# Last slots of a pixart block: maxima in the ring's banks, transposed scores over four banks, remainders last in a projection

## The chip, the core and the metric

The kernel runs on one core of one Trainium2 chip, in one launch. The metric is the time of one execution in device microseconds (us), and the median of several executions is given. The engines are TensorE (PE, whose loads of the stationary operand have a row of their own, PEld), VectorE (DVE), ScalarE (ACT), GpSimd (POOL) and SyncE (SP, which issues nearly all DMAs).

## The reference, cut to what matters

A transformer block over B = 16 batches of N = 256 tokens with H = 256 features, 16 heads of 16 features each, and an MLP of width 1024, all in float32:

```
x  = x + gate_a * (softmax(q k^T / 4) v @ W_proj + b_proj)      q, k, v from ln(x) @ W_qkv     "s"
x  = x + softmax(qc kc^T / 4) vc @ W_cproj + b_cproj            qc from ln(x), kc, vc from ln(context)   "c"
x  = x + gate_m * (gelu(ln(x) @ W_mlp1 + b_mlp1) @ W_mlp2 + b_mlp2)
```

The softmax of the reference subtracts the row's maximum. The kernel does so too, with a maximum taken over the tokens of each head.

## The kernel before, in words

Every projection splits each operand in a high and a low part and sums three products (high by high, high by low, low by high). The low part of an activation comes from a subtraction that follows the high part: for the attention's output `xTh_ac` is written by ACT, then `y_ac` (the unsplit copy) by ACT, then `xTl_ac` = `y_ac` - `xTh_ac` by POOL.

**Units, visits and beats.** The attention work is a list of 32 units: 16 of kind "s" and 16 of kind "c", one batch each. Units 28 to 31 are the context attentions of batches 12 to 15. `beat(n, k)` is the body of two nested loops, `n` from -1 to 31 and `k` from 0 to 7; in the text "visit (n, k)" is its first part, `visit(n, k, home)`. A visit does two things side by side. For unit n+1 it computes one token half of four heads' scores (`s_tile`, two partition halves `par` of 63 rows, 4 matmuls named `s<-big`), and DVE reduces their maxima into `mx` (`mx<-s`). For unit n it computes transposed scores of two heads (`t_part`, 4 matmuls named `st<-big`), and ACT exponentiates all four tiles in one instruction (`exp`, written to `pt`). The maxima are wanted as a 64th row of the stacked queries, so that the second matmul subtracts them: `m_part` transposes half of `mx` on PE (`psm`), ACT negates it into `m`, and SP sends it into `big`. That happens for unit n's second half at k = 0 and for unit n+1's first half at k = 4.

**PSUM.** There are eight banks. `sp` (two banks, the scores for the maxima) and `st` (two banks, the transposed scores) are fixed and single: the scores of a visit can't be written before the reduction of the visit before has read `sp`, nor the transposed scores before the `exp` of the visit before has read `st`. The other four are two rings of two: `LONG` (projections of the next units, later the MLP's first layer `ph`) and `SHORT` (everything brief: `psm`, the attention's output `o`, transposes `psA_c` and `psT_ac`, the output projection `psP_c`, and `ps_warm`, idle matmuls that `busy` puts in at given slots).

**The rest of a beat.** k = 0 and k = 4 run `av_part`, the product with the values (`o`, 32 matmuls). k = 2 and k = 6 transpose the output (`post.turn`, `psA_c`), `norm` divides by the row sum (DVE: reciprocal `rc_c`, then `A_c`), k = 4 transposes `A_c` (`psT_ac`) and makes the high part, k = 5 the low part. For the last four units (`whole = n > nu - 4`) the output projection is done in one piece, `p1.proj(0)` and `p1.proj(1)` at k = 6, with `end`, `add` and `store` at k = 7. Before, each call of `proj(t)` takes one token half, and in it the products follow one another as high-high, high-low, low-high for each of the two slices of the features. The last unit's projection runs in the MLP's loop instead, one call in each step (list `pst` after the loop over beats).

**The MLP.** It follows the attention, 16 batches of four chunks: `mlp_first` (`ph`, 12 matmuls), two gelus on ACT (`hf`, `hh`), a subtraction on POOL (`hl`), `mlp_second` (12 matmuls into `sp` or `st` by turns of the batch, named `s<-big,hh` and `st<-big,hh`). The first four chunks' `mlp_first` and the first batches' layer norms (`x`, `st_m`, `rs_m`, `xn_m`, `psT_m`, `xTf_m`) are put into the last attention beats.

Every engine's instructions are kept in program order, so the order on each queue is the one written out here. All calls go through one helper, so the profile gives line L51 for every operation; the names of the tiles tell them apart.

Of the kernel before, what the change touches and what calls it, by code (L numbers as in the profile page):

```python
# [16 lines left out]
P = 128  # L17
# [4 lines left out]
def pixart_block(  # L22
# [8 lines left out]
    B, N, H = x.shape  # L31
# [3 lines left out]
    NT = N // P  # L35
    KC = H // P
# [20 lines left out]
    PE = InOrder(nc.tensor, True)  # L57
# [7 lines left out]
    LONG, SHORT = "gen", "tr"  # L65
    ps_turn = [0]

    def ps_gen(name, tag=None):


        if tag is None and ps_turn[0] is not None:
            ps_turn[0] ^= 1
            tag = (SHORT, LONG)[ps_turn[0]]
        tag = tag or SHORT
        return psum.tile([P, 512], F32, tag=tag, name=name, bufs=2)
# [22 lines left out]
    def tok(ap, b):  # L98
        return ap[b].rearrange("(t p) h -> p t h", p=P)
# [33 lines left out]
    st = psum.tile([P, 2, 512], F32, tag="st", name="st", bufs=1)  # L133
    sp = psum.tile([P, 2, 512], F32, tag="s", name="s", bufs=1)
# [227 lines left out]
    def mm3_tok(dst, xT, t, W, kn=KC, start=True, stop=True):  # L362
        n = 0
        for k in range(kn):
            for a, b in ((xT[0], W[0]), (xT[0], W[1]), (xT[1], W[0])):
                PE.matmul(dst, a[:, k, t * P:(t + 1) * P], b[:, k],
                          start=(start and n == 0), stop=(stop and n == 3 * kn - 1))
                n += 1
# [120 lines left out]
    def bc_t(ap):  # L489
        return ap.unsqueeze(1).to_broadcast([P, NT, H])  # L490
# [25 lines left out]
    def build_post(u):  # L516

        b, name = u.b, f"{u.kind}{u.b}"
        W = Wp if u.kind == "s" else Wcp
        o = Box()  # L520

        def begin():
            if u.kind == "c":
                return
            G[b] = work.tile([P, 2, H], F32, tag="g", name=f"g_{b}", bufs=3)
            SP.dma_start(G[b].rearrange("p a h -> p (a h)"),
                         gd[b, 0:2].rearrange("a h -> (a h)").partition_broadcast(P))

        def gate():
            if u.kind == "c":  # L530
                return
            o.xg = work.tile([P, NT, H], F32, tag="xg", name=f"xg_{b}")
            POOL.tensor_tensor(o.xg, X[b], bc_t(G[b][:, 1]), ALU.add)

        def turn(hf):
            o.ps = ps_gen(f"psA{hf}_{name}", SHORT)
            for t in range(NT):
                for r in range(2):
                    PE.transpose(o.ps[:, (2 * t + r) * P:(2 * t + r + 1) * P],
                                 u.oT[hf][:, r, t * P:(t + 1) * P], ident)  # L540

        def norm(hf):
            if hf == 0:
                o.A = work.tile([P, NT, H], F32, tag="A", name=f"A_{name}", bufs=1)
            pv = o.ps.rearrange("p (x h c) -> p x h c", x=4, h=4)
            rc = work.tile([P, 4, 4, 1], F32, tag="rc", name=f"rc{hf}_{name}")
            DVE.reciprocal(rc, pv[:, :, :, HD:HD + 1])
            A = o.A.rearrange("p t (r f) -> p (t r) f", r=2)[:, :, 64 * hf:64 * hf + 64]
            DVE.tensor_tensor(A.rearrange("p x (h i) -> p x h i", h=4),
                              pv[:, :, :, 0:HD], rc.to_broadcast([P, 4, 4, HD]), ALU.mult)  # L550

        aT = transposed(lambda: o.A, f"a{name}", pool=True)

        def proj(t):
            if t == 0:
                o.ps = ps_gen(f"psP_{name}")
            mm3_tok(o.ps[:, t * H:(t + 1) * H], aT.xT, t, W)

        def end():
            t1 = work.tile([P, NT, H], F32, tag="t1", name=f"t1_{name}")  # L560
            o.t1 = t1
            ACT.copy(t1.rearrange("p t h -> p (t h)"), o.ps)

        def add():
            t1 = o.t1
            if u.kind == "s":
                POOL.tensor_tensor(t1, t1, bc_t(G[b][:, 0]), ALU.mult)
                X1[b] = work.tile([P, NT, H], F32, tag="x1", name=f"x1_{b}", bufs=5)
                POOL.tensor_tensor(X1[b], o.xg, t1, ALU.add)
            else:  # L570
                POOL.tensor_tensor(t1, t1, X1[b], ALU.add)
                o.out = t1

        def store():
            if u.kind == "c":
                SP.dma_start(tok(X2d, b), o.out)

        o.W, o.src, o.tok, o.name = W, aT, True, f"P_{name}"
        o.aT, o.begin, o.gate, o.turn, o.norm, o.proj, o.end, o.add, o.store = aT, begin, gate, turn, norm, proj, end, add, store
        u.post = o  # L580
        o.hurry = u.kind == "s" and b in (0, B - 1)
# [7 lines left out]
    def s_tile(u, g, par, t, bank=None, home=sp):  # L589

        alone = bank is None
        if alone:
            turn_of_s[0] ^= 1
            bank = turn_of_s[0]
        apart = isinstance(home, tuple)
        for j in range(2):
            PE.matmul((home[bank] if apart else home[:, bank])[:, j * N:(j + 1) * N],
                      u.q[par * 64:par * 64 + 63, 2 * g + j, t * P:(t + 1) * P],  # L600
                      u.k[par * 64:par * 64 + 63, 2 * g + j, :], start=True, stop=True)
            if j == 0:
                yield
        if u.mx is None:
            u.mx = work.tile([P, 2, 2, 4, NT], F32, tag="mx", name=f"mx_{u.n}", bufs=3)
        mx = u.mx.rearrange("p f r a t -> p r f a t")
        a = slice(2 * (g % 2), 2 * (g % 2) + 2)
        if alone or apart:
            src = home[bank] if apart else sp[:, bank]
            DVE.tensor_reduce(mx[:, par, g // 2, a, t], src.rearrange("p (j n) -> p j n", j=2),  # L610
                              AX.X, ALU.max)
        elif bank == 1:
            DVE.tensor_reduce(mx[:, :, g // 2, a, t], home.rearrange("p r (j n) -> p r j n", j=2),
                              AX.X, ALU.max)
        yield
# [8 lines left out]
            SP.dma_start(u.q[par * 64 + 63:par * 64 + 64, 4 * hf:4 * hf + 4, :].bitcast(F32),  # L624
                         m[par * 8:(par + 1) * 8].bitcast(F32))

    def t_part(u, pair, par):


        for c in range(NT):  # L630
            PE.matmul(st[:, par, c * N:(c + 1) * N],
                      u.k[par * 64:par * 64 + 64, pair, c * P:(c + 1) * P],
                      u.q[par * 64:par * 64 + 64, pair, :], start=True, stop=True)
            if c == 0:
                yield
        yield

    def exp(u, pair):
        u.pt[pair] = work.tile([P, 2, NT, N], F32, tag="pt", name=f"pt_{u.n}_{pair}", bufs=5)
        ACT.activation(u.pt[pair].rearrange("p r c n -> p (r c n)"), st.rearrange("p r n -> p (r n)"),  # L640
                       AF.Exp, scale=SCALE)

    later = []
# [7 lines left out]
    def in_turn(*pieces):  # L651

        for _ in range(2):
            for f in pieces:
                next(f)
# [23 lines left out]
    units = []  # L679
    for n, (kind, b) in enumerate(seq):  # L680
        u = Box()
# [5 lines left out]
    nu = len(units)  # L687
# [174 lines left out]
    for n, v in (("0", u0), ("1", u1), ("2", u2)):  # L862
        for c in "KQV":
            o = getattr(v, c)
# [8 lines left out]
    for n, v in (("0", u0), ("1", u1), ("2", u2)):  # L873
        word["T" + n + "t"], word["T" + n + "h"], word["T" + n + "l"] = v.T[0].parts
        word["T" + n + "p"] = v.T[0].low_pool
        for c in "KQ":
            o = getattr(v, c)
# [51 lines left out]
    def unit(n):  # L929
        return units[n] if 0 <= n < nu else None  # L930

    def visit(n, k, home=sp):


        v, e = unit(n + 1), k
        s = []
        if v:
            s = [s_tile(v, e // 2, par, e % 2, par, home) for par in range(2)]
        if n < 0:
            in_turn(*s)  # L940
            return
        t = [t_part(units[n], k, par) for par in range(2)]
        in_turn(*s)
        in_turn(*t)
        later.append(lambda: exp(units[n], k))

    def beat(n, k):
        if n < 0:
            visit(n, k, (st, sp)[k % 2])
            return  # L950
        cur, prev, nxt = unit(n), unit(n - 1), unit(n + 1)
# [22 lines left out]
        if k == 6 and q2:  # L974
            q2.V.keep()
        light = k == 6 and nxt and 3 < n < nu - 4 and not lx
        visit(n, k, (sp[:, 0], ps_gen("s1", SHORT)) if light else sp)
        if k == 0:
            if cur:
                m_part(cur, 1)  # L980
# [103 lines left out]
    for n in range(-1, nu):  # L1084
        ACT.on = E_['ON'][0] or n >= nu - 1
        for k in range(8):
            beat(n, k)
            for f in at[n, k]:
                f()
            if (n - nu, k) in W1P:  # L1090
                next(w1, None)
            if (n - nu, k) in W2P:
                next(w2, None)
            for q in (2 * k, 2 * k + 1):
                for f in at_end[n - nu, q]:
                    f()
# [3 lines left out]
    o = last.post  # L1100
# [78 lines left out]
```

## Time and profile before

| what | value |
|---|---|
| median of 3 runs | 810.0 us (808.59 to 810.6) |
| the profiled execution, its time | 807.08 us |
| its span, first to last instruction | 805.3 us |
| its mean granted TensorE clock | 0.999 |
| PE busy in the span | 781.0 us (97%) |
| DVE, ACT, POOL busy | 595.7, 584.9, 465.6 us |
| last units (about 560 to 621 us): PE busy | 53.72 of 61.00 us |

The profiled execution is 1.78 us longer than its span (start and end of the launch), and 2.9 us under the median of the runs. The visits that the change touches lie between 561 and 605 us, and the last unit's projection at 616 to 621 us. A row of the timeline gives the start, the time taken, the engine, the operation with its tiles, how many instructions were merged into it, and in brackets how long the engine sat idle before it and what ended that.

### The profile page before, as it was taken

To read this page: it belongs to the slowest core of one execution; us is meant where nothing else is said; L and a number is where in the kernel's file an instruction comes from. 1 tells how busy PE (TensorE), PEld (TensorE's weight loads), DVE (VectorE), ACT (ScalarE), POOL (GpSimd) and SP (SyncE) were. 2 spreads that over 40 slices of the span, in tenths; PEclk is the share of its full clock that TensorE was granted. 3 is DMA by queue.
4 is the path that set the end of the run, shared out by engine and by line. 5 is a ranking of instruction groups with operands and counts; after the bars stand their busy time and mean duration, and the time that the engine had idled before them with its cause. 6 is when DMAs were issued, how large, how long until landed. Compare 5 with 4: busy or idle time off the path is not lost.

```text
span 805.3 us, 23708 instructions
## 1 busy us (share of the span) xinstructions
PE 781.0 (97%) x9455; PEld 659.1 (82%) x9455; DVE 595.7 (74%) x1058; ACT 584.9 (73%) x1024; POOL 465.6 (58%) x405
## 2 busy tenths in 40 slices
PE   9999999999999999999999999999889999999997
PEld 8687777878877787877787787877568999999997
DVE  4887878788887878878888888876663666666662
ACT  3368878878888887888888888887556666666663
POOL 5755737574463756546475676663445666666653
PEclk9999999999999999999999999999999999999999
DMA  6554443435344443534445454534211312211311
GB/s 204 138 166 109 120 130 109 127 97 150 99 134 116 134 124 109 154 95 136 112 126 153 126 153 120 148 100 128 82 42 42 92 57 63 80 56 64 80 42 51
DMA packets 89939, 87.88 MB, mean 109 GB/s; under 512 B 9507, under 2 KB 85573, under 8 KB 89829
## 3 DMA queue, kind: packets, MB, share of 16 engines
q1 hardware_dynamic: 89364, 85.58, 38.0%
q8 instruction: 75, 1.23, 0.6%
q0 software_dynamic: 192, 0.52, 0.2%
q14 instruction: 36, 0.29, 0.1%
q10 hardware_dynamic: 272, 0.26, 0.1%
HBM read 26.97 MB, written 8.46 MB: 44 GB/s over the span
## 4 chain that ended last, share of the span: by engine, by line
PE 74%; DVE 11%; issue 5%; POOL 4%; ACT 4%; DMA 2%; SPq 0%; POOLq 0%; ACTq 0%
PE s L51 15%; PE o L51 13%; PE ph L51 11%; PE st L51 11%; DVE mx L51 8%; PE ps_qc L51 3%; PE ps_kc L51 3%; PE ps_q L51 3%; PE ps_P_s L51 2%; ACT pt L51 2%; PE ps_v_s L51 2%; PE psm L51 1%; PE ps_v_c L51 1%; PE ps_k L51 1%; PE ps_P_c L51 1%
## 5 line engine op out<-in xcount | busy, mean ns | idle before, releaser
L51 DVE TENSOR_REDUCE mx<-s 128x4 f32<-128x1024 f32 (+1 forms) x262 | 309.0, 1182 | 95.7 <-PE s L51 92.8
L51 ACT ACTIVATE pt<-st 128x1024 f32<-128x1024 f32 x256 | 261.1, 1020 | 45.4 <-PE st L51 38.7
L51 PE MATMUL s<-big 63*128 63x256 f32 x1008 | 120.2, 309 | 9.0 <-DVE mx L51 6.5
L51 PE MATMUL o<-pt,v 128*32 128x256 f32 x2048 | 123.8, 382 | 0.0
L51 POOL TENSOR_TENSOR hl<-hf,hh 128x512 fp32r<-128x512 f32 x64 | 88.7, 1395 | 55.7 <-ACT hh L51 54.7
L51 PEld LDWEIGHTS s<-big 63*128 63x128 f32 x1008 | 80.0, 185 | 43.8 <-DVE mx L51 22.7
L51 PE MATMUL st<-big 64*128 64x256 f32 (+1 forms) x1040 | 110.2, 284 | 3.6 <-ACT pt L51 3.6
L51 PEld LDWEIGHTS o<-pt,v 128*32 128x32 f32 x2048 | 60.0, 109 | 40.8
L51 PEld LDWEIGHTS st<-big 64*128 64x128 f32 (+1 forms) x1040 | 83.2, 186 | 8.2 <-ACT pt L51 6.1
L51 ACT ACTIVATE hf<-ph,bT 128x256 f32<-128x256 f32 x120 | 50.6, 474 | 27.8 <-PE ph L51 27.8
L51 ACT ACTIVATE hh<-ph,bT 128x256 fp32r<-128x256 f32 x120 | 50.5, 471 | 24.9 <-PE s L51 13.1
L51 ACT COPY oT<-o 128x512 f32<-128x512 f32 x63 | 37.0, 587 | 42.4 <-PE o L51 42.4
L51 POOL TENSOR_TENSOR xTl_c<-y_c,xTh_c 128x512 fp32r<-128x512 f32 x16 | 20.5, 1281 | 60.2 <-PE s L51 52.0
L51 POOL TENSOR_TENSOR xTl_as<-y_as,xTh_as 128x512 fp32r<-128x512 f32 x16 | 20.5, 1278 | 56.1 <-ACT y_as L51 56.1
L51 PE MATMUL ph<-wqch,wself 128*128 128x256 f32 x256 | 51.8, 285 | 0.0
L51 PE MATMUL ph<-wkch,wself 128*128 128x256 f32 x256 | 51.8, 286 | 0.0
L51 POOL TENSOR_TENSOR xTl_ac<-y_ac,xTh_ac 128x512 fp32r<-128x512 f32 x16 | 20.5, 1280 | 54.0 <-ACT y_ac L51 50.1
L51 PE MATMUL s<-big,hh 128*128 128x256 f32 x256 | 47.4, 282 | 0.0
L51 PE MATMUL st<-big,hh 128*128 128x256 f32 x256 | 47.2, 281 | 0.0
L51 DVE TENSOR_SCALAR xn_m<-x,mv_m,rs_m 128x256 f32<-128x256 f32 x32 | 38.3, 1235 | 11.4 <-POOL rs_m L51 11.4
L51 PEld LDWEIGHTS ph<-wqch,wself 128*128 128x128 f32 x256 | 42.0, 191 | 0.4 <-issue 0.4
L51 PEld LDWEIGHTS ph<-wkch,wself 128*128 128x128 f32 x256 | 41.9, 191 | 0.4
(222 smaller groups left out, 2379.0 us busy)
## 6 DMA issues: line engine op xcount, KB each, us to landing
big<-h_kc SPq DMA_DIRECT2D x64, 128.0 KB
big<-h_qc SPq DMA_DIRECT2D x64, 128.0 KB
big<-h_k SPq DMA_DIRECT2D x62, 128.0 KB
big<-h_q SPq DMA_DIRECT2D x62, 128.0 KB
big<-l_k SPq DMA_DIRECT2D x32, 128.0 KB
big<-l_q SPq DMA_DIRECT2D x32, 128.0 KB
c<-in_ctx_dram SPq DMA_DIRECT2D x16, 256.0 KB
g<-gd SPq DMA_DIRECT2D x16, 256.0 KB
```

The costliest lines, as they stand in the source:

```text
L51: i = f(*a, **k)
```

## The change

There are three edits.

1. Maxima: in every second visit from (29, 7) on, namely (29, 7), (30, 1), (30, 3), (30, 5) and (30, 7), the two tiles of scores go into the two `LONG` banks instead of `sp`. With two separate tiles the reduction is done by two instructions of 128x512 in place of one of 128x1024 (`apart` in `s_tile`).
2. Transposed scores: in the last unit (n = 31, which has no scores for maxima beside it), odd visits write to `sp` and even ones to `st`, and `exp` reads that bank.
3. Whole projections: `proj(0)` now does the eight matmuls with the high part for both token halves, and `proj(1)` the four with the low part, as one accumulation group in the bank. It applies to units 28, 29 and 30 (at k = 6 of the beat after) and 31 (in the MLP's loop: `proj(0)` before `mlp_second` of chunk 2, `proj(1)` after it).

```diff
-        def proj(t):
-            if t == 0:
+        def proj(half):
+
+            if half == 0:
                 o.ps = ps_gen(f"psP_{name}")
-            mm3_tok(o.ps[:, t * H:(t + 1) * H], aT.xT, t, W)
+            for t in range(NT):
+                for k in range(KC):
+                    for a, b in (((1, 0),) if half else ((0, 0), (0, 1))):
+                        PE.matmul(o.ps[:, t * H:(t + 1) * H], aT.xT[a][:, k, t * P:(t + 1) * P], W[b][:, k],
+                                  start=(half == t == k == b == 0), stop=(half == 1 and t == NT - 1 and k == KC - 1),
+                                  skip_group_check=True)
...
+        bank = sp if n == nu - 1 and k % 2 else st
+        t = [t_part(units[n], k, par, bank) for par in range(2)]
...
+        later.append(lambda: exp(units[n], k, bank))
...
-        visit(n, k, (sp[:, 0], ps_gen("s1", SHORT)) if light else sp)
+        home = sp
+        if light:
+            home = sp[:, 0], ps_gen("s1", SHORT)
+        elif nxt and n * 8 + k >= nu * 8 - 17 and k % 2:
+            home = ps_gen("s0", LONG), ps_gen("s1", LONG)
+        visit(n, k, home)
```

`t_part` and `exp` take the bank as an argument `st` that stands for the tile of that name.

More of the change, by code (lines that the diff above doesn't have):

```diff
@@ L625, in m_part, with t_part @@
                          m[par * 8:(par + 1) * 8].bitcast(F32))
-    def t_part(u, pair, par):
+    def t_part(u, pair, par, st):
         for c in range(NT):
@@ L636, in t_part, with exp @@
         yield
-    def exp(u, pair):
+    def exp(u, pair, st):
         u.pt[pair] = work.tile([P, 2, NT, N], F32, tag="pt", name=f"pt_{u.n}_{pair}", bufs=5)
@@ L941, in visit @@
             return
-        t = [t_part(units[n], k, par) for par in range(2)]
+        bank = sp if n == nu - 1 and k % 2 else st
+        t = [t_part(units[n], k, par, bank) for par in range(2)]
         in_turn(*s)
         in_turn(*t)
-        later.append(lambda: exp(units[n], k))
+        later.append(lambda: exp(units[n], k, bank))
     def beat(n, k):
```

## The prediction

> **What bounds the kernel now.** I read the page's busy row first, then busy time by stretch, then PE's waits in the stretch that the change touches, then the timeline there.
>
> ```profile
> 100.00:540.00 440.00, 433.78 (x6138) 347.85 (x6128) 364.04 (x627) 362.73 (x581) 256.81 (x223) 1.00 0.45 125
> 560.00:621.00 61.00, 53.72 (x523) 41.85 (x521) 35.14 (x71) 36.37 (x55) 28.89 (x24) 1.00 0.20 61
> 621.00:806.00 185.00, 179.13 (x1484) 176.25 (x1482) 105.87 (x196) 110.26 (x262) 108.65 (x86) 0.99 0.22 64
> ```
>
> The columns are the stretch, its length, then busy us of PE, PEld, DVE, ACT and POOL, PE's granted clock, DMA share and GB/s. PE is full in the attention (434 of 440) and in the MLP (PE ends at 800.4; until then the waits show 0.2 us of idle PE and 2.9 us of PEld). Only the last units have holes, 7.3 us. What PE gains there therefore reaches the end.
>
> ```profile
> engine line waited for: us in total, times, longest us
> PEld s L51 <- DVE mx L51: 4.1, 5, 1.4
> PEld psP_c L51 <- POOL xTl_ac L51: 2.8, 4, 1.4
> PEld st L51 <- ACT pt L51: 2.2, 2, 1.4
> ```
>
> These are PEld's waits from 561 to 621 us: scores wait for the reduction that frees `sp`, projections for the remainder, transposed scores for the exponential that frees `st`. Together 9.1 us, and each edit aims at one row. The timeline says how much of each is real gain:
>
> ```profile
> 564.80 0.40 PE L51 MATMUL st<-big 64*128 64x256 f32 x4
> 566.29 0.57 PE L51 MATMUL s<-big 63*128 63x256 f32 x4 [1.09 <-DVE mx L51]
> 566.63 0.46 PE L51 MATMUL st<-big 64*128 64x256 f32 x4
> ...
> 574.06 0.40 PE L51 MATMUL st<-big 64*128 64x256 f32 x4
> 575.70 0.50 PE L51 MATMUL s<-big 63*128 63x256 f32 x4 [1.24 <-DVE mx L51]
> 576.04 0.40 PE L51 MATMUL st<-big 64*128 64x256 f32 x4
> ...
> 593.72 0.50 PE L51 MATMUL st<-big 64*128 64x256 f32 x4 [0.59 <-ACT pt L51]
> ...
> 616.59 0.28 PE L51 MATMUL psP_c<-wcpl,xTh_ac 128*128 128x256 f32 x1
> 618.07 0.38 PE L51 MATMUL psP_c<-wcph,xTl_ac 128*128 128x256 f32 x1 [1.20 <-POOL xTl_ac L51]
> ```
>
> Behind each delayed `s` stands an `st`, and that needs the exponential of the visit before, which releases almost as late:
>
> ```profile
> 565.30 1.02 ACT L51 ACTIVATE pt<-st 128x1024 f32<-128x1024 f32 x1 [2.20 <-PE st L51]
> 574.56 1.02 ACT L51 ACTIVATE pt<-st 128x1024 f32<-128x1024 f32 x1 [0.91 <-PE st L51]
> ```
>
> It starts 0.50 after its `st` and takes 1.02; the next `st` starts 0.05 later (586.54 to 586.59). From `st` to `st` that makes 1.57, where the reduction makes 1.83 (564.80 to 566.63) and 1.98.
>
> **Edit 3, remainders last.** Twelve matmuls come 0.12 apart. Now the third waits; afterwards the ninth does, 0.72 later.
> - Unit 28 (562.3): second matmul 562.52, third 563.07 where 562.64 was possible, and a restart takes 0.22 to the next instead of 0.12. The remainder ends at 563.03, the ninth is due at 563.36. Gain 0.43 + 0.10 = 0.53.
> - Unit 29 (582.4): 583.29 against 582.77, 0.62 in full. But PE will by then be 2.0 early (below), and the remainder is not: POOL must first do the split `big<-w` (1.27) that follows a cast on DVE, which I find only 0.86 early. POOL then ends the remainder near 581.6, the ninth is due at 581.5. Gain 0.40.
> - Unit 30 (602.3): 603.00 against 602.66, plus 0.10: 0.44.
> - Unit 31 (616.5): 618.07 against 616.71, plus 0.10: 1.46. In place of the wait stand six matmuls and `mlp_second` of chunk 2, whose `hl` ends at 616.79 and is thus in time; the remainder is needed only after it.
>
> Sum 2.83. Nothing is added on any engine.
>
> **Edit 1, maxima.** DVE pays for five pairs:
>
> ```profile
> L51 DVE TENSOR_REDUCE mx<-s 128x4 f32<-128x1024 f32 x242 | 296.1, 1223 | 95.6 <-PE s L51 92.8
> L51 DVE TENSOR_REDUCE mx<-s 128x2 f32<-128x512 f32 x20 | 12.9, 686 | 0.0
> ```
>
> Ten such pairs are in the trace already (20 instructions, 12.9 us): 1.29 a pair against 1.22, so 0.07 more. [...]
>
> Place by place, with the saving carried forward (0.53 from unit 28):
> - (30, 0): `s` goes at once, `st` waits for the exponential: 1.57 in place of 1.83, gain 0.26. Then `psm` takes the bank that `A_c` frees. On DVE `A_c` ends 1.84 after the reduction's start, 1.91 with a pair, about 566.4; PE would be there at 566.2. Loss 0.15. Saved so far 0.64.
> - (30, 2): idle 0.22 before `s` goes, and the exponential (570.16 to 571.18) frees `st` before 571.26. Gain 0.22, so far 0.86.
> - (30, 4): 1.98 becomes 1.57, gain 0.41, so far 1.27. `psm` needs the pair of (30, 3): DVE is 0.86 early, so it ends at 573.57 + 1.29 = 574.86; `psm` is due at 575.10.
> - (30, 5): the reduction before was held up behind `st_m<-x`, which waits for POOL. PEld idles 0.68 before `s`, of which 0.17 is issue after transposes: gain 0.51, so far 1.78.
> - (30, 6): 0.22, so far 2.00; with unit 29's projection 2.40.
> - (31, 0): the wait of 1.17 for the exponential stays (even visit, same bank). `psm` waits for `A_c` here too: loss 0.07.
>
> Sum 1.40 of the row's 4.1. The ring is free: its last user, `v<-ps_v_c`, ends at 562.15. New on PE's path is the landing of `l_qc` for the first scores of unit 31: the trace has it at 563.90, `s` of (30, 0) will want it at 564.6. The row `m` of (30, 4) landed at 573.73 with its issue now 0.5 earlier; wanted at 574.8. No gap either way: at 0 here, and if the landing were 1 us later, 0.3 and 0 lost.
>
> **Edit 2, four banks.** Only (31, 3) waits among the odd and later visits: PEld idle 0.83, gone in full, as `sp`'s exponential (31, 1) ended 4 us before. So far 2.33 + 0.83 = 3.16. What is late next? `psT_m` of batch 1 at 598.85 needs `xn_m`, at the end of a chain: `x2d<-t_c` on SP 588.56, two `m` DMAs behind it, `x<-x2d` 590.43, POOL `x` 593.17, `st_m`, `rs_m`, `xn_m` ending 597.21. It starts from unit 29's projection, so it moves 2.33 to 594.9; PE arrives at 595.7. Margin 0.8, cost 0.
>
> **Sum.** 2.83 + 1.40 + 0.83 = 5.06, say 5.1 us. The profiled execution would go from 807.08 to 802.0. The median of the runs stands 2.9 above that execution, and I carry the saving over: 810.0 - 5.1 = 804.9.
>
> TensorE's clock: the trace grants 1.0 from 4.2 to 802.9 us and 0.5 from there, 2.5 after the last matmul (800.4). Waits up to 1.2 cost no clock; the change shortens them. [...]
>
> **The rivals.**
> - *The chain to `xn_m` does not move* (its DMA is bound by something else on SP's queue). Then `psT_m` goes at 597.25, not 595.7: 1.6 lost, 3.5 gained, 806.5. For it: a chain of waits that follows exactly these steps up to `xn_m` at 596.4. Against: each step in it is released by the one before, none by a clock of its own. Chance 0.10.
> - *Waits only change names:* exponentials take the maxima's place fully (gain 0 of 1.40), (31, 3) passes its 0.83 on to `o`, and unit 31's 1.46 is given back to the gelus, whose `hh` is what `ph` of the next batch waits for. Left 1.4, 808.6, no change that can be told: a measurement here tells 0.3%, 2.4 us. Against: `hh` of chunk 5 waits for `mlp_second` of chunk 2, which comes earlier too. Chance 0.05.
> - *Slower:* one transfer that PE meets earlier, the `x<-x2d` of batch 1, lands late among others. Its place is `psT_m` in (31, 4). A wait past 2.5 us would also drop the clock to 0.5, as at the end; the record has the full clock only from 4.2 us after the start, so I estimate half of that, 2 us, for a drop. It turns the sum negative when `xn_m` comes over 3.1 later than before (597.2): wait 1.6 + 3.1 = 4.7, plus 2, against 5.1; at 5 later, 1.6 + 5 + 2 - 5.1 = 3.5 slower, 813.5. Against: DMA share there is 0.10 to 0.36. Chance 0.05.
> - That edit 1 does nothing is excluded: the program has the five pairs in those visits.
>
> **Numbers.** My case has 0.80: 804.9, with its own range 803.3 to 806.2 (DVE's and POOL's lateness up to 1.3 worse; landings and waits up to 1.6 better, short of the 9.1 less the 1.4 that stays). With the first rival and the runs' scatter of 1 us: 803.0 to 807.5. Faster by over 0.3%: 0.80 + 0.10 = 0.90; same 0.05; slower 0.05.
>
> **What would show it.** In the profile after, between 561 and 621 us: PEld's waits for `mx` gone but for some tenths; its waits for `pt` up to 2.5, at (30, 0), (30, 4) and (31, 0); for `xTl_ac` under 0.4; the first `psT_m` after the last projection at 615.7 in place of 620.8; pairs of 0.69 in five visits. Wrong would be: `psm` waiting over 0.5 for DVE, `psT_m` of batch 1 waiting for `xn_m`, a granted clock under 1.0 before 795, or an MLP that doesn't start earlier.

## The result and the profile after

The median went from 809.27 us (6 runs, 808.59 to 810.6) to 804.81 us (6 runs, 802.47 to 805.27); the ratio is 0.9941 with a 95% interval of 0.993 to 0.9953. The forecast was 804.9. An execution with a low mean granted clock (one of edit 3 alone had 0.853 and took 844.89 us) is left out of all ratios here. The profiled execution took 804.78 us with a span of 803.0 us, only 2.3 less than the one before. Which of the two numbers is the change's? The exponentials of one visit ahead of the first edit give the answer, first before and then after (timelines of ACT):

```profile
562.07 1.02 ACT L51 ACTIVATE pt<-st 128x1024 f32<-128x1024 f32 x1
```

```profile
564.46 1.03 ACT L51 ACTIVATE pt<-st 128x1024 f32<-128x1024 f32 x1
```

This is visit (29, 6). The execution after reached it 2.39 us later, with the same program up to there; the exponentials of units 27 to 29 stand 2.38 to 2.45 apart, and 1.1 of it is there at the first exponential. It is what two executions differ by in their first 500 us, and belongs to no edit. So I measure the **tail**: from that exponential to the end of the last matmul. It is 238.29 us before (562.07 to 800.37) and 233.58 after (564.46 to 798.04): 4.71 us less, near the 4.46 that the medians differ by. Up to the last projection the tail tells executions apart to a few hundredths (where two versions have the same code, they agree to 0.01), and at its end to about 0.1, which a time with 2 us of scatter can't.

Busy time by stretch after (columns as in the prediction; moved by the 2.39, the stretch that was 560 to 621 before would be 562.4 to 618.7, which has the same holes as the second row):

```profile
100.00:540.00 440.00, 433.90 (x6133) 348.28 (x6129) 363.19 (x625) 362.82 (x582) 254.95 (x223) 1.00 0.45 125
560.00:616.00 56.00, 52.42 (x535) 40.58 (x528) 36.64 (x79) 35.03 (x50) 25.07 (x22) 1.00 0.24 74
616.00:806.00 190.00, 181.83 (x1507) 178.96 (x1505) 105.85 (x196) 113.23 (x270) 112.32 (x89) 0.99 0.21 62
```

PE's holes in the last units shrank from 7.3 to 3.6 us. Of the three rows of PEld's waits from 561 to 621 us one remains (sum, number, longest):

```profile
PEld st L51 <- ACT pt L51: 3.7, 3, 1.4
```

And one of PE's own waits in the same stretch, with the same columns:

```profile
PE psm L51 <- DVE A_c L51: 0.3, 2, 0.2
```

The rows for `mx` (4.1) and `xTl_ac` (2.8) are gone, and the one for `pt` grew from 2.2 to 3.7, with three waits, two of them new. The timeline of PE shows where:

```profile
566.89 0.41 PE L51 MATMUL s<-big 63*128 63x256 f32 x4
568.24 0.50 PE L51 MATMUL st<-big 64*128 64x256 f32 x4 [0.94 <-ACT pt L51]
568.91 0.27 PE L51 MATMUL psm<-ident,mx 128*16 128x128 f32 x1 [0.17 <-DVE A_c L51]
...
577.37 0.50 PE L51 MATMUL st<-big 64*128 64x256 f32 x4 [0.94 <-ACT pt L51]
577.80 0.28 PE L51 MATMUL psm<-ident,mx 128*16 128x128 f32 x1
...
586.82 0.50 PE L51 MATMUL st<-big 64*128 64x256 f32 x4 [1.18 <-ACT pt L51]
...
593.32 0.50 PE L51 MATMUL s<-big 64*128 64x256 f32 x4
...
616.46 0.28 PE L51 MATMUL psP_c<-wcpl,xTh_ac 128*128 128x256 f32 x1
...
618.02 0.64 PE L51 MATMUL psP_c<-wcph,xTl_ac 128*128 128x256 f32 x4
618.50 0.60 PE L51 MATMUL psT_m<-ident,xn_m 128*128 128x128 f32 x4
```

At (30, 0) and (30, 4) `s` goes at once, and `st` behind it waits 0.94 where `s` had waited 1.09 and 1.24: most of the maxima's wait only moved one instruction on. At (31, 3) the transposed scores, now in `sp` and so named `s` (593.32), wait for nothing, and neither does the last unit's remainder (618.02), with `mlp_second` ahead of it. The last row is the start of the MLP's steady part. It came at 620.81 before, which is 623.20 with the 2.39 added; so 4.70 of the 4.71 are there by then, and the MLP passes them on to the end.

### The profile page after: what moved, and what is told of

It is laid out like the page before. It is cut to its first block, busy times and chain, and to the rows that moved or that the text cites. A ratio compares the mean times of both kernels' runs of the same rounds, so it can differ in the third digit from the quotient of the medians.

```text
span 803.0 us, 23712 instructions
## 1 busy us (share of the span) xinstructions
PE 781.8 (97%) x9455; PEld 660.3 (82%) x9455; DVE 596.0 (74%) x1063; ACT 584.8 (73%) x1024; POOL 465.4 (58%) x405
## 4 chain that ended last, share of the span: by engine, by line
PE 79%; DVE 9%; ACT 4%; POOL 3%; issue 3%; DMA 1%; ACTq 0%; POOLq 0%; SPq 0%
PE s L51 17%; PE o L51 14%; PE ph L51 11%; PE st L51 11%; DVE mx L51 7%; PE ps_qc L51 3%; PE ps_kc L51 3%; PE ps_q L51 3%; ACT pt L51 2%; PE ps_P_s L51 2%; PE ps_v_s L51 2%; PE ps_v_c L51 2%; PE psm L51 2%; PE ps_k L51 1%; PE ps_P_c L51 1%
## 5 line engine op out<-in xcount | busy, mean ns | idle before, releaser
L51 ACT ACTIVATE pt<-st 128x1024 f32<-128x1024 f32 x252 | 257.0, 1020 | 40.3 <-PE st L51 34.1
L51 PE MATMUL s<-big 63*128 63x256 f32 (+1 forms) x1024 | 122.1, 309 | 6.5 <-DVE mx L51 3.6
L51 PEld LDWEIGHTS s<-big 63*128 63x128 f32 (+1 forms) x1024 | 81.2, 185 | 41.6 <-DVE mx L51 19.0
```

Of the source, the lines that this page charges most:

```text
L51: i = f(*a, **k)
```

## The experiments

All savings below are from the tail of one profiled execution of each version, place by place: the start of the exponential of a visit, counted from that of (29, 6), in us earlier than before. The rows are cumulative.

| saved by the start of | after | edit 3 alone | edit 1 alone | edit 2 alone | `norm` early | flipped | both |
|---|---|---|---|---|---|---|---|
| exp (29, 7) | 0.53 | 0.53 | 0.00 | 0.00 | 0.53 | 0.53 | 0.53 |
| exp (30, 0) | 0.51 | 0.54 | -0.02 | 0.00 | 0.74 | 0.51 | 0.74 |
| exp (30, 4) | 0.96 | 0.53 | 0.43 | 0.00 | 1.20 | 0.95 | 1.20 |
| exp (30, 6) | 1.61 | 0.52 | 1.08 | 0.00 | 1.84 | 1.60 | 1.84 |
| exp (30, 7) | 2.17 | 1.16 | 0.94 | 0.00 | 2.40 | 2.15 | 2.39 |
| exp (31, 0) | 2.12 | 1.15 | 0.88 | 0.00 | 2.58 | 2.10 | 3.05 |
| exp (31, 3) | 2.78 | 1.15 | 0.88 | 0.66 | 3.24 | 2.77 | 3.39 |
| exp (31, 7) | 3.23 | 1.60 | 0.87 | 0.67 | 3.68 | 3.21 | 3.83 |
| last projection done | 4.69 | 3.06 | 0.87 | 0.66 | 5.14 | 4.67 | 5.29 |
| last matmul done | 4.71 | 3.05 | 0.78 | 0.66 | 5.13 | 4.66 | 5.28 |

**Edit 3 alone** (the kernel before with the new `proj`):

```diff
-        def proj(t):
+        def proj(half):
...
-            mm3_tok(o.ps[:, t * H:(t + 1) * H], aT.xT, t, W)
+            for t in range(NT):
+                for k in range(KC):
+                    for a, b in (((1, 0),) if half else ((0, 0), (0, 1))):
```

> Only edit 3 (remainders last). The tail is measured from the exponential of visit (29, 6) to the end of the last matmul: 238.3 us before, 233.6 with all three edits, 4.7 less. Theory (each projection's wait is real gain, nothing behind it gives it back): 0.53 + 0.62 + 0.44 + 1.46 = 3.05 us less in the tail, so 235.25; unit 29 gains its full 0.62 here, since PE is only 0.53 early there and POOL's remainder moves by as much. Time about 806.2 against 809.3. Rival (waits only change names: what units 28 to 30 save is lost again at the next wait for maxima or exponentials): 1.5 us less, 236.8. In the rows: waits of PEld for xTl_ac gone, those for mx (4.1) and pt (2.2) as before.

Median 806.46 against 809.48, ratio 0.9962 (0.9948 to 0.9977), 3.1 us less by the ratio. The rows are those of another execution, profiled at a mean granted clock of 0.998:

> The same kernel with edit 3 alone, for a profile at full clock. Theory: 3.05 us less in the tail (235.25) with steps of 0.53, 0.62, 0.44 and 1.46 at the four projections. Rival (lost again at the next wait): 236.8, with steps that vanish at (30, 0) and (31, 0).

Its tail is 3.05 us shorter, with steps of 0.53, 0.63, 0.44 and 1.46. The waits for `mx` (4.1) and `pt` (2.2) are unchanged. The theory holds, the rival falls: these four waits, with nothing behind them that another engine holds back, are gain in full.

**Edit 1 alone** (the kernel before with the new `home`):

```diff
-        visit(n, k, (sp[:, 0], ps_gen("s1", SHORT)) if light else sp)
+        home = sp
...
+        elif nxt and n * 8 + k >= nu * 8 - 17 and k % 2:
+            home = ps_gen("s0", LONG), ps_gen("s1", LONG)
+        visit(n, k, home)
```

> Only edit 1 (maxima of every second visit in the ring). Theory: the after trace shows 1.15 us gained at (30, 0) to (30, 6) and a loss of 0.04 at (31, 0); alone, unit 29's projection stands in the way, because its third matmul waits for a remainder that ACT's y_ac allows only about 0.9 earlier. So 0.9 us less in the tail, between 0.7 and 1.1: 237.4. Time about 808.4. Rival (exponentials take the place of the maxima fully): 0.3 or less. Rival (maxima are worth the 1.4 forecast): 1.4. In the rows: PEld's wait for mx from 4.1 to under 0.5, its wait for pt from 2.2 to about 4, the wait for xTl_ac larger than 2.8 by 0.2 to 0.5.

The tail is 0.87 shorter at the last projection and 0.78 at the end, within the 0.7 to 1.1. The times can't tell it: ratio 0.9995 (0.9984 to 1.0007). PEld's waits in this run:

```profile
PEld st L51 <- ACT pt L51: 4.5, 4, 1.4
PEld psP_c L51 <- POOL xTl_ac L51: 3.0, 4, 1.4
```

The wait for `mx` (4.1 before) is gone, and 2.3 of it is back under `pt`. At unit 29's projection 1.08 falls to 0.94, where the third matmul waits for its remainder: this is why edit 1 is worth 0.97 by (31, 0) beside edit 3 (2.12 against the 1.15 of edit 3 alone) and 0.88 without. In unit 30 itself it is worth 1.08 in both.

**Edit 2 alone:**

```diff
+        bank = sp if n == nu - 1 and k % 2 else st
+        t = [t_part(units[n], k, par, bank) for par in range(2)]
...
+        later.append(lambda: exp(units[n], k, bank))
```

> Only edit 2 (transposed scores over four banks in the last unit). Theory: the 0.67 us that the after trace shows at (31, 3) come alone as well, since everything behind starts from PE: 0.67 less in the tail, 237.6; time about 808.6, hard to tell from no change by the clock, but the tail tells it. Rival (the chain that ends in xn_m of batch 1, or the wait for o, takes it back): under 0.2 less. In the rows: PEld's wait for pt from 2.2 to 1.4, the one at (31, 0) left.

The tail is 0.66 shorter, all of it at (31, 3), and nothing gives it back. The ratio, 0.9993 (0.9981 to 1.0006), can't tell. The wait for `pt` fell from 2.2 to 1.4, the one at (31, 0). The three edits alone make 3.05 + 0.78 + 0.66 = 4.49, together 4.71; at the last projection, ahead of the MLP's scatter, it is 4.59 against 4.69.

**What holds psm: `norm` early, the banks flipped, both.** In the changed kernel `psm` at (30, 0) and (31, 0) waits for `A_c`, whose bank of the `SHORT` ring it takes. `norm` early:

```diff
+        if k == 7 and cur and whole:
+            cur.post.norm(0)
         home = sp
...
-            if cur:
+            if cur and not whole:
                 cur.post.norm(0)
```

> The changed kernel, with norm(0) of units 29 to 31 issued ahead of the scores of visit (n, 7) instead of behind its reduction: the bank that psm waits for is then free earlier. Theory: psm of (30, 0) and (31, 0), which the after trace shows waiting 0.17 for A_c behind pairs of reductions, goes right after its st: 0.34 and 0.33, so 0.67 less in the tail than the changed kernel (233.6 to 232.9); time about 804.1. Rival (psm waits for the pair itself): 0.1 or less at (30, 0), where the pair ends at 568.14 and st starts at 568.24.

Tail 233.17 (5.13 less), so 0.42 more, 0.23 at each place where 0.34 and 0.33 were expected; median 804.26, ratio 0.9935 (0.9916 to 0.9954). The wait was real, its size off by 0.1: behind an `st` that has waited itself, `psm` follows 0.43 later (587.05 to 587.48 here), not 0.33 as behind one that hadn't.

```diff
-        bank = sp if n == nu - 1 and k % 2 else st
+        bank = sp if n == nu - 1 and k % 2 == 0 else st
```

> The changed kernel, with the banks of the last unit the other way round (sp in even visits, st in odd ones), so that the transposed scores of (31, 0) need not wait 1.18 for the exponential of (30, 7). Theory: the wait moves from st to psm, which A_c holds at the same place: the tail stays at 233.6 within 0.1, although the largest wait of PEld for pt is gone. Rival (the exponential is the bound): 1.2 less, 232.4.

Tail 233.63, 0.05 longer than the changed kernel's; median 804.63. The timeline of PE around (31, 0):

```profile
584.89 0.39 PE L51 MATMUL s<-big 64*128 64x256 f32 x4
586.90 0.27 PE L51 MATMUL psm<-ident,mx 128*16 128x128 f32 x1 [1.62 <-DVE A_c L51]
```

The transposed scores (now in `sp`) wait for nothing, and `psm` 1.62 instead. A wait of 1.18 was taken away and bought nothing: the next one, of `psm` for `A_c`, ends where it did.

> Both: norm(0) early and the banks flipped. Theory: at (31, 0) psm is then held by the pair of reductions alone, which ends 0.76 before psm starts now: 0.72 there and 0.34 at (30, 0), 1.06 less in the tail than the changed kernel (232.5), more than the 0.67 and 0.0 of the two alone; time about 803.7. Rival (the parts add up): 0.67 if the exponential does not matter, 1.9 if it does.

Tail 233.01, 0.57 less than the changed kernel's; median 804.1, ratio 0.9932 (0.991 to 0.9955). The same place:

```profile
583.54 0.40 PE L51 MATMUL s<-big 64*128 64x256 f32 x4
584.84 0.28 PE L51 MATMUL psm<-ident,mx 128*16 128x128 f32 x1 [0.90 <-DVE mx L51]
585.36 1.93 PE L51 MATMUL o<-pt,v 128*32 128x256 f32 x32 [0.24 <-ACT t_c L51]
```

`psm` is held by the pair of reductions, as expected, and starts 0.94 earlier than in the changed kernel (where it gained 2.12 on before, here 3.06). But 0.32 of it is lost in the next instruction, which takes the bank that ACT's copy `t_c` of the projection reads. So the two together gain more than apart (0.57 against 0.42 - 0.05), less than the 1.06 forecast.

**The idle matmuls.** Groups of `ps_warm` fill PE at five slots of units 30 and 31. Without them:

```diff
-... (30, 0): 'd3', (30, 1): 'd2', (30, 2): 'd3', (30, 5): 'd3', (31, 1): 'd2'
```

> The changed kernel without the idle matmuls ps_warm of (30, 0), (30, 1), (30, 2), (30, 5) and (31, 1): 26 matmuls, 3.7 us of PE, whose output nothing reads. Theory (with the maxima's wait gone, unit 30 is held by the chain of exponential, reduction and psm, not by PE): only about 1.4 of the 3.7 come back, 0.8 by (31, 0) and 0.6 at (31, 1); tail 232.2, time about 803.4; waits of PEld for pt and of psm for DVE appear in unit 30. Rival (PE is the bound there): 3.7 less, 229.9. Rival (the idle matmuls hold the clock): granted clock under 1.0 in some stretch from 565 to 600 us and a time that is no better.

Up to (31, 0) the tail is 3.07 shorter than before, 0.95 more than in the changed kernel: the chain of exponential, reduction and `psm` keeps the rest, as the theory said. Then more than that gain goes. The timeline of PE:

```profile
587.02 3.62 PE L51 MATMUL o<-pt,v 128*32 128x256 f32 x32
```

And the busy time in the 5 us around it (columns as above; the granted clock is the third from the end):

```profile
585.00:590.00 5.00, 3.69 (x36) 1.83 (x37) 3.69 (x7) 2.67 (x4) 2.61 (x3) 0.71 0.16 53
```

The 32 matmuls `o` take 3.62 in place of 1.93, and the granted clock in those 5 us is 0.71; the trace has it at 0.5 from 587.1 to 590.5. By (31, 1) the saving is 1.40, and the tail ends at 234.01, 0.43 longer than the changed kernel's. The second rival is right for this execution as far as its signs go; whether the missing groups did it is another matter, since the 3.4 us ahead of the fall hold none of the five slots (last section). (Median 804.19, ratio 0.9935, 0.9915 to 0.9956.)

On top of `norm` early and the flip, three groups taken out, then all five:

```diff
-(30, 0): 'd3', (30, 1): 'd2', (30, 2): 'd3'
```

> The version with norm(0) early and the banks flipped (tail 233.0, 5.3 less than before), and without the idle matmuls of (30, 0), (30, 1) and (30, 2); those of (30, 5) and (31, 1) stay. Theory: as in the run without any of them, the chain of unit 30 gives back about 0.9 of their 2.3 us, and with the waits of (31, 0) gone the clock stays at 1.0: tail 232.1, time about 803. Rival (unit 30's waits let the clock fall, as in that run): a stretch at 0.5 between 565 and 595 us, tail 233.5 or more.

Again the clock fell, earlier: 0.5 from 575.7 to 579.2. The busy time around that:

```profile
575.00:580.00 5.00, 4.05 (x40) 1.94 (x39) 3.51 (x9) 2.08 (x3) 3.20 (x3) 0.66 0.06 18
```

The saving was 2.00 at (30, 3) and 1.37 at (30, 5); tail 233.39, no better than with the groups (233.01). Median 803.63, ratio 0.9919 (0.9894 to 0.9944).

> The same without any of the five groups of idle matmuls. Theory: 0.6 more at (31, 1): tail 231.5, time about 802.4, if the clock holds. Rival (it does not hold, as in the run without them): a stretch of 3.4 us at 0.5, which costs 1.7, tail 233.2, and runs that spread more widely than those of the other versions.

Here the clock held in the profiled execution (1.00 in each stretch of 5 us from 560 to 605, 0.999 in the mean), and the theory's number came out: tail 231.50, 6.79 less than before and 2.08 less than the changed kernel. The median is 802.5, ratio 0.9921 (0.9894 to 0.9947), the lowest median here, though the version with three groups out has the same ratio (0.9919); its eight runs spread from 800.78 to 808.32, over 7 us, where the changed kernel's spread over 2.8. By the times it isn't told apart from the changed kernel (the intervals overlap).

How often does the clock fall? The mean granted clock of a whole execution is 0.997 in both profiled ones where it fell and 0.998 to 1.0 in the others profiled at full clock, so I take 0.997 or less for the sign of a fall; that is my estimate from these means. It was recorded for 9 of the 20 runs of the three versions with groups left out and for 2 of the 25 of the four changed versions with all groups, but also for 13 of the 53 of the kernel before and for 5 of the 11 of edit 1 alone, which have all groups too. So by this sign a fall is likelier without the groups than in the changed versions with them, but they don't exclude it.

## Why the prediction was right

That the median was forecast to 0.1 us is luck: the median of before that I started from was 0.7 above the one it was compared with (810.0 against 809.27), and the saving was forecast 0.6 above what the medians gave (5.06 against 4.46), so the two errors cancelled. What can be judged are the terms, which add to 5.06 against 4.71 in the tail. Term by term, with every visit's exponential counted as in the table's column "after":

| term | forecast | measured |
|---|---|---|
| remainder, unit 28 | 0.53 | 0.53 |
| (30, 0): wait moved, less `psm` | 0.26 - 0.15 | -0.02 |
| (30, 2) | 0.22 | 0.14 |
| (30, 4) | 0.41 | 0.31 |
| (30, 5) | 0.51 | 0.51 |
| (30, 6) | 0.22 | 0.14 |
| remainder, unit 29 | 0.40 | 0.56 |
| (31, 0), `psm` | -0.07 | -0.05 |
| (31, 3), four banks | 0.83 | 0.66 |
| remainder, unit 30 | 0.44 | 0.44 |
| remainder, unit 31 | 1.46 | 1.46 |

- **Remainders**: exact where nothing else moves. Unit 29's was 0.16 better than forecast: PE was only 1.61 early at that point, not 2.0, so of the 0.22 that I had charged for POOL's lateness 0.07 showed (0.56 against 0.63 with edit 3 alone).
- **Maxima**: the mechanism was the one forecast (`st` waits for the exponential instead, `psm` for `A_c`), the sizes 0.1 too kind at four places. At (30, 0) I let `psm` start as `A_c` ends; in the profile after it starts 0.15 later (568.76 to 568.91). At (30, 4) the cost is the 0.43 from a waiting `st` to `psm` against 0.33. At (30, 2) and (30, 6) I had the exponential free `st` in time; it ended 0.05 ahead of `st` (573.70 and 573.75 at (30, 2)), which is the distance at the places that wait, and what stands behind `st` came 0.44 after it in place of 0.34. One sign was missed with this: the row for `pt` was to stay under 2.5 and is 3.7, at the three places named.
- **Four banks**: I took the whole 0.83 of PEld's idle time, and forgot the 0.17 of issue that follows transposes, which I had subtracted at (30, 5). With it the term is 0.66, as measured.
- **The first rival** (the chain to `xn_m` stays): it moved with unit 29's projection. In the profile after, `xn_m` of batch 1 ends at 597.30 and `psT_m` starts at 598.44: margin 1.1, cost 0. **The second** (waits only change names) is half true of edit 1, where 2.3 of 4.1 came back under another name in the run with edit 1 alone, and false of the other two edits. **The third** didn't happen: the clock was 1.00 from 7.0 to 802.3 us.
- **DVE's price** for a pair: 1.29 (at 566.85 and 585.43), as in the ten pairs of before (20 instructions, 12.9 us), 0.07 more than a single reduction (1.22).
- **The clock**: the prediction said that waits of up to 1.2 us cost none, and that one past 2.5 would. The first held in the changed kernel's profile (waits of up to 1.18, clock 1.00), but is no rule: in two versions the clock fell after waits of PE of 1.18 and 0.95 at most in the 3.4 us ahead. The second was an estimate from the end of the program and was not shown: the longest wait of PE in the profiles around the edits is 1.62 (flipped banks, with the clock at 1.00). Nor is 2.5 a bound, for from the last matmul to the fall at the end it took 2.5 us in the profile before (800.37 to 802.90) and 4.3 in the one after (798.04 to 802.33).

## What to carry to other kernels

Ask of each wait on the busiest engine what releases the instruction *behind* it: the maxima's 4.1 us of waits held 1.0 us of gain, because the next instruction waited for something almost as late, while the remainders' 2.8 us of waits held all of it and the restarts too (3.05 with edit 3 alone). When a step is made of parts of which one comes late, put that part last in the whole group, not last in each piece. And to tell savings below a run's scatter, count from an instruction ahead of the edit to the end of the last one, and read the saving place by place.

## What the runs showed of the hardware

The clock of TensorE fell to half without any long gap. In the two profiled executions (0.997 in the mean) where it fell ahead of the program's end, it was at 0.5 for 3.4 us, and in the 3.4 us ahead of that PE's longest waits were 1.18 and 0.95 us; PE was busy in them for 2.05 and 2.26 us. The busy time in the stretch ahead of the fall, with all five groups left out:

```profile
583.70:587.10 3.40, 2.05 (x21) 1.39 (x25) 2.39 (x6) 1.50 (x2) 1.73 (x2) 1.00 0.00 0
```

The same with three groups left out, on top of `norm` early and the flip:

```profile
572.30:575.70 3.40, 2.26 (x20) 1.55 (x20) 3.33 (x9) 2.09 (x3) 0.66 (x1) 1.00 0.41 136
```

PE's busy share alone doesn't tell these stretches from others: some of the same length, in which PE was no busier than in the second, kept the clock. This is one of the version with flipped banks, with the clock at 1.00 in it and 0.999 in the mean of the execution:

```profile
585.52:588.93 3.41, 2.03 (x33) 1.02 (x33) 3.25 (x7) 2.31 (x4) 1.27 (x1) 1.00 0.00 0
```

The kernel before (2.12 us, 584.45 to 587.86) and the changed kernel (2.23 us, 583.88 to 587.29) have such stretches too, and their clock stays at 1.00 until 802.90 and 802.33. And the stretch ahead of the fall with all five groups left out (583.70 to 587.10) lies between the slots (30, 5) and (31, 1): the groups could only shift the work in time, not fill that stretch.

The record of the full clock runs from 4.18 to 802.90 us in the profile before and from 7.03 to 802.33 in the one after. That is 798.72 and 795.31 us, or 234 and 233 times 3.413, and the falls lasted 3.4. It looks as if the clock changed in steps of that length, but this is my estimate from two profiles and two falls. Counted in such steps from the start of the record, the stretch of the kernel before is the 171st and that of the changed kernel the 170th.

So the clock fell after stretches that were 60% and 66% busy, while others with 60%, 62% and 65% kept it. What decides between them, no run here shows.
